# A relational graph network on one core: 128 counted nodes in the first layer, and all counted products in one pass over the row blocks

## The chip, the core and the metric

The kernel runs on one core of a Trainium2 chip. Its engines work side by side and meet at semaphores: TensorE (PE in the profile) multiplies, VectorE (DVE) and ScalarE (ACT) work element by element, GpSimd (POOL) issues the gathers, and SyncE (SP) issues most other transfers. [...]The metric is the device time of one execution in microseconds.

## The reference, cut to what matters

```
src, dst, type: 100000 edges; dst = int(6250 * u^2), sorted; x: 6250 x 256
for l in range(3):                        # W_rel[l]: 8 x 256 x 256
    xr  = einsum('nd,rde->rne', x, W_rel[l])
    agg = segment_sum(xr[type, src], dst, 6250)
    x   = relu(agg + x @ W_root[l] + bias[l])
x = layernorm(x_in + x)
x = layernorm(x + attention(x, edges))    # four heads, the attention runs at the end
```

A layer sums, for each node and each of the 8 relations, the rows of the edges that arrive there, and multiplies the sums by that relation's weights. Because `dst` is a square of a uniform number, nodes with low numbers get very many edges: the first 64 nodes get about 10,100 of the 100,000, the first 128 about 14,300, the first 192 about 17,500.

## The kernel before, in words

**Edges in tiles.** The 782 tiles of 128 sorted edges are worked off in groups of four, one group per step of the loop at the end of `layer`, from the last tile down to the first. Tiles above and below `TM` are interleaved and have two separate accumulators `S[0]` and `S[1]` (rings of node tiles, f = 0 and f = 1). In a step, `gather` (L577) lets POOL fetch the source rows of four tiles into one of the seven buffers of `msg` (rows split into three bf16 parts; in the first 32 steps of layer zero, unsplit f32); `onehot` (L557) compares keys on DVE; `windows` (L597) multiplies rows by one-hots on PE into a window of W nodes by 8 relations; `add` (L609) adds the windows to `S` on DVE at a place read at run time. When a node tile of 128 nodes has all its edges (the table `ready` says after which step), `dense` (L664, L668) multiplies its sums by the weights: 18 f32 matmuls, which the trace records as 36, dealt out a few per step, or one node tile per step once the groups are used up. `finish` adds the bias, applies relu, and stores the row block twice, as f32 (L703) and as three bf16 parts (L706). The next layer's gathers take any row, so they start after the last store.

**Hot nodes are counted.** For the first `HOTS[l]` nodes of a layer (64, 192, 192) no edge is gathered; the tiles that hold only such edges are skipped. `starts` and `count` build instead, for 64 nodes at a time (a chunk), a table of how many edges come from each row under each relation: per pair of a node and 128 of its edges, a compare on DVE (L897; every fourth pair one more, L893), a matmul (L905), and per node a copy by ACT to the byte array `A` (L908). The table is written to device memory (`cnts`, L914). `products` then multiplies all rows of the layer by the counts: 13 row blocks of up to 512 rows, per chunk two products (k = 0, 1) of eight matmuls of 512 columns (L993), rows split into two parts `top` and `rest` (L976 on ACT, L977 on DVE), counts cast to f32r by ACT (L981), and a sum on DVE (L960). A row block is loaded (L949) into a buffer of `msg`, the pool of the gathers.

**Where this work stands.** `jobs` is a generator that the loop asks up to three times a step (`work(0)` ahead of the gather, `work(1)` after the windows, `work(2)` after the adds). What it yields names the places at which it may go on; at HEAVY, a product is given out only where the planner's tally of PE time lies below 5 us times the step, or where the products left outnumber 0.9 times the steps left to `last_step`:

```
def light(i):
    return spent[0] < STEP * i + SLACK or left[0] > 0.9 * (last_step - i)
last_step = (PREP_AT if final else NG) - 12
```

Layer zero counts chunk 0 (steps 44 to 97), does its 26 products (98 to 134, straight from `A`), then counts chunk 1 (150 to 183, past its last group). Layer one counts chunk 2 (12 to 34) and does 78 products in two passes, chunks 0 and 1 first and then chunk 2, which loads and splits every row block twice (39 to 153). Layer two does the same two passes (10 to 141). Node tile 0 has no gathered edges in layers one and two; its dense work then comes at `ready[1, 1] - 2`, two steps before the last group.

Of the kernel before, what the change touches and what calls it, by code (L numbers as in the profile page):

```python
# [29 lines left out]
PAD = 32  # L30
MARGIN = 800
CHUNK = 64
HOTS = (64, 192, 192)
PASSES = ((0, 1), (2,))
FIRST = 32
SELS = 6
LOWS = 3
# [138 lines left out]
def fast(tc, const, pl, x, xs, xb, src, dst, edge_type, w_rel, w_root, bias, weight,  # L176
# [10 lines left out]
    with ExitStack() as top:  # L187
# [35 lines left out]
        with ExitStack() as s:  # L223
            wp = s.enter_context(tc.tile_pool(name="wp", bufs=1))
            sp = s.enter_context(tc.tile_pool(name="sp", bufs=1))
            xp = s.enter_context(tc.tile_pool(name="xp", bufs=3))
            hp = s.enter_context(tc.tile_pool(name="hp", bufs=1))
            ps_w = s.enter_context(tc.tile_pool(name="ps_w", bufs=4, space=PSUM))
            ps_d = s.enter_context(tc.tile_pool(name="ps_d", bufs=1, space=PSUM))
            ps_h = s.enter_context(tc.tile_pool(name="ps_h", bufs=2, space=PSUM))  # L230

            mp = s.enter_context(tc.tile_pool(name="mp", bufs=7))
            op = s.enter_context(tc.tile_pool(name="op", bufs=AHEAD + 2))

# [43 lines left out]
def tables(tc, pl, ps_t, src, dst, edge_type, ident, idx, key, pos, iota, iota_p, lane, edges, hd,  # L278
# [5 lines left out]
    with tc.tile_pool(name="prep", bufs=1) as prep:  # L284
# [120 lines left out]
        masked = prep.tile([P, 64], F32, name="masked")  # L405
        for h, k, t0, t1 in (
                (HOTS[-1], key1, pl.THS[-1], pl.K1),
                (HOTS[0], key[:, pl.TH:pl.bands[0][1]], pl.TH, pl.bands[0][1])):
# [114 lines left out]
def layer(tc, pl, l, final, groups, ready, S, hold, A, hd, key1, edges, cnts, flag, idx, key, pos, iota,  # L523
# [303 lines left out]
    def count(chunk, pace=ALL):  # L827
# [58 lines left out]
        for m in range(len(pairs) + SELS - 2):  # L886
# [14 lines left out]
            if m >= SELS - 2:  # L901
# [4 lines left out]
                if i == rows_[n] - 1:  # L906
# [20 lines left out]
    def products():  # L927

        B = GT
        C = CHUNK * R  # L930
        assert C == 512
        loads = [range(a, min(a + B, NT)) for a in range(0, NT, B)]
        sums = hp.tile([P, 2, KC, C], F32, name="sums")
        room = A.rearrange("p j s -> p (j s)")
        more = room[:, :4 * KC * C].bitcast(F32).rearrange("p (k c) -> p k c", k=KC)
        kept = [room[:, 4 * KC * C + i * 2 * B * C:4 * KC * C + (i + 1) * 2 * B * C] for i in range(2)]
        held_ = {}

        def load(m, cs):
            js = loads[m]  # L940
            t = mp.tile([P, GT, 3 * D], BF16, name="msg").rearrange(
                "p q d -> p (q d)").bitcast(F32)[:, :B * D].rearrange("p (q d) -> p q d", d=D)
            full = len(js) if js[-1] < NT - 1 or LAST == P else len(js) - 1
            if full < len(js):
# [6 lines left out]
            for u, c in enumerate(cs if l else ()):  # L951
                nc.sync.dma_start(kept[m % 2][:, u * B * C:u * B * C + len(js) * C],
                                  cnts[c][:, js[0] * C:(js[-1] + 1) * C])
            return t

        def add_up(m, o, ph):
            if m == 0:
                nc.vector.tensor_copy(o, ph[:, :C])
            else:
                nc.vector.tensor_tensor(o, o, ph[:, :C], ALU.add)  # L960

        for cs in PASSES:
            cs = [c for c in cs if c < HOT // CHUNK]
            if not cs:
                continue
            for c in cs:
                held_[c] = sums[:, c] if c < 2 else more
            ts = {0: load(0, cs)}
            yield from pause(3)
            yield MID  # L970
            last = None
            for m, js in enumerate(loads):
                g = len(js)
                t = ts.pop(m)
                top, rest = buffer(0, F32R, B * D), buffer(1, F32R, B * D)
                nc.scalar.copy(top[:, :g * D], t[:, :g].rearrange("p t d -> p (t d)"))  # L976
                nc.vector.tensor_tensor(rest[:, :g * D], t[:, :g].rearrange("p t d -> p (t d)"),  # L977
                                        top[:, :g * D], ALU.subtract)
                for u, c in enumerate(cs):
                    cn = buffer(2, F32R, B * C)  # L980
                    nc.scalar.copy(cn[:, :g * C], kept[m % 2][:, u * B * C:u * B * C + g * C] if l  # L981
                                   else room[:, js[0] * C:(js[-1] + 1) * C])
                    if u == 0 and m + 1 < len(loads):
                        ts[m + 1] = load(m + 1, cs)
                    for k in range(KC):
                        if last:
                            yield END
                            add_up(*last)
                        yield HEAVY
                        ph = ps_h.tile([P, 512], F32, name="ph")  # L990
                        for n in range(g):
                            for part in (top, rest):
                                nc.tensor.matmul(  # L993
                                    ph[:, :C], part[:, n * D + k * P:n * D + (k + 1) * P],
                                    cn[:, n * C:(n + 1) * C], start=(n == 0 and part is top),
                                    stop=(n == g - 1 and part is rest))
                        last = m, held_[c][:, k], ph
                        left[0] -= 1
                    yield MID
            add_up(*last)  # L1000
            yield HEAD
        while not {3, 4} <= set(cleared):
            yield HEAD
        for c, v in held_.items():
            j, at = divmod(c * CHUNK, P)
            for k in range(KC):
                o = cols(1, j)[:, k * R:(k + 1) * R, at:at + CHUNK]
                nc.vector.tensor_tensor(
                    o, o, v[:, k].rearrange("p (n r) -> p r n", r=R), ALU.add)
        summed.append(True)  # L1010
        yield HEAD

# [722 lines left out]
```

## Time and profile before

| | us |
|---|---|
| median of three runs (lowest, highest) | 3454.05 (3449.44, 3460.27) |
| the profiled execution, its own time | 2871.54 |
| its span, first to last instruction | 2869.7 |
| PE / DVE / POOL / ACT busy in the span | 2503.9 / 1925.6 / 1955.1 / 847.7 |
| mean granted PE clock | 0.945 |

The profile is of one execution, and its time is well below the median of the runs; durations below are those of the profiled execution. A group in the profile has its line, engine and operation, the tile written and the tiles read, the number of instructions, the busy time, the mean of one in ns, and then the idle time of the engine before them with what ended it. A timeline row gives the start, the length, the engine, the line, and in brackets the idle time before it.

### The profile page before, as it was taken

To read this page: it belongs to the slowest core of one execution; us is meant where nothing else is said; L and a number is where in the kernel's file an instruction comes from. 1 tells how busy PE (TensorE), PEld (TensorE's weight loads), DVE (VectorE), ACT (ScalarE), POOL (GpSimd) and SP (SyncE) were. 2 spreads that over 40 slices of the span, in tenths; PEclk is the share of its full clock that TensorE was granted. 3 is DMA by queue.
4 is the path that set the end of the run, shared out by engine and by line. 5 is a ranking of instruction groups with operands and counts; after the bars stand their busy time and mean duration, and the time that the engine had idled before them with its cause. 6 is when DMAs were issued, how large, how long until landed. Compare 5 with 4: busy or idle time off the path is not lost.

```text
span 2869.7 us, 55366 instructions
## 1 busy us (share of the span) xinstructions
PE 2503.9 (87%) x20054; PEld 2168.5 (76%) x20055; DVE 1925.6 (67%) x4564; ACT 847.7 (30%) x1178; POOL 1955.1 (68%) x2026
## 2 busy tenths in 40 slices
PE   2899999999766689999999998789999999998775
PEld 1788778787655578888888877678888888877664
DVE  6776888767655468666666766367666665767858
ACT  2332223333123224332333342212222232232014
POOL 5657777777777477677777777477767766667701
PEclk8999999999989799999999999899999999999885
DMA  5756666766666666767676776566656665666724
GB/s 156 229 189 184 191 187 185 237 212 212 177 183 176 198 176 189 244 201 213 211 229 210 216 249 201 156 211 179 199 176 190 195 202 171 215 200 195 236 71 159
DMA packets 245854, 560.53 MB, mean 195 GB/s; under 512 B 43533, under 2 KB 124452, under 8 KB 245188
## 3 DMA queue, kind: packets, MB, share of 16 engines
q0 software_dynamic: 126656, 387.18, 46.3%
q1 hardware_dynamic: 115720, 166.95, 17.0%
q8 instruction: 161, 2.64, 0.4%
q10 hardware_dynamic: 3196, 2.76, 0.3%
q14 instruction: 121, 0.99, 0.1%
HBM read 492.51 MB, written 64.21 MB: 194 GB/s over the span
## 4 chain that ended last, share of the span: by engine, by line
PE 60%; DVE 12%; issue 8%; DMA 7%; POOL 6%; ACT 5%; SPq 2%; DVEq 1%; ACTq 0%; POOLq 0%
PE pd L668 27%; PE pw L597 16%; PE ph L993 10%; POOL msg L577 6%; DMA msg<-xb,idx 4%; PE pd L664 4%; DVE S L609 3%; ACT S L682 1%; ACT u L981 1%; PE pw L641 1%; SPq L850 1%; PE ph L905 1%; DMA u<-in_x_dram 1%; DVE oh L557 1%; DMA u<-in_dst_dram 1%
## 5 line engine op out<-in xcount | busy, mean ns | idle before, releaser
L577 POOL DMA_INDIRECT msg<-xb,idx x1886 | 1823.4, 967 | 704.0 <-issue 536.4
L668 PE MATMUL pd<-wr,S 128*128 128x256 f32 x4800 | 1123.2, 384 | 1.6 <-DVE S L650 1.1
L609 DVE TENSOR_TENSOR S<-S,pw 128x320 f32 (+21 forms) x2010 | 848.7, 422 | 391.8 <-PE pw L597 262.8
L668 PEld LDWEIGHTS pd<-wr,S 128*128 128x128 f32 x4800 | 904.8, 192 | 119.3 <-DVE S L650 2.1
L597 PE MATMUL pw<-oh,msg 128*128 128x160 bf16 (+20 forms) x11316 | 746.3, 224 | 150.7 <-DMA msg<-xb,idx 124.6
L597 PEld LDWEIGHTS <-msg 128*128 128x128 bf16 x11316 | 679.7, 101 | 245.9 <-DMA msg<-xb,idx 149.7
L993 PE MATMUL ph<-u,u 128*128 128x512 f32 x1372 | 380.1, 418 | 36.6 <-ACT u L981 36.3
L557 DVE TENSOR_TENSOR oh<-iota,key 128x640 bf16<-128x640 f32 (+19 forms) x475 | 319.4, 673 | 16.4 <-issue 12.4
L993 PEld LDWEIGHTS ph<-u,u 128*128 128x128 f32 x1372 | 256.3, 193 | 92.4 <-ACT u L981 41.4
L682 ACT ACTIVATE S<-S 128x2048 uint32<-128x2048 uint32 x150 | 284.5, 1896 | 4.3 <-PE pd L668 2.6
L644 ACT COPY xT<-pw 128x256 f32<-128x256 f32 x195 | 71.8, 371 | 682.2 <-PE pw L641 682.2
L664 PE MATMUL pd<-wo,xT 128*128 128x256 f32 x588 | 168.4, 411 | 27.0 <-DVE h L710 20.2
L981 ACT CAST u<-A 128x2048 fp32r<-128x2048 uint8 (+1 forms) x91 | 163.5, 1797 | 50.4 <-PE ph L993 38.7
L577 POOL DMA_INDIRECT msg<-in_x_dram,idx x124 | 120.3, 970 | 77.4 <-issue 31.7
L908 ACT CAST A<-ph 128x392 uint8<-128x392 f32 x192 | 90.9, 485 | 272.4 <-PE ph L905 268.2
L698 ACT ACTIVATE hb<-h 128x256 bf16<-128x256 f32 x98 | 41.1, 419 | 413.5 <-DVE h L697 413.5
L977 DVE TENSOR_TENSOR u<-msg,u 128x1024 fp32r<-128x1024 f32 (+1 forms) x65 | 75.6, 1163 | 130.4 <-ACT u L976 130.3
L664 PEld LDWEIGHTS pd<-wo,xT 128*128 128x128 f32 x588 | 107.5, 200 | 43.9 <-DVE h L710 22.5
L597 PE MATMUL pw<-A,msg 128*128 128x120 f32 (+5 forms) x496 | 85.8, 330 | 29.0 <-DVE S L609 21.6
L716 ACT ACTIVATE rs<-mv,eps 128x1 f32<-128x1 f32 x49 | 14.4, 295 | 309.0 <-DVE mv L715 308.0
L597 PEld LDWEIGHTS pw<-A,msg 128*128 128x128 f32 x496 | 78.7, 207 | 34.9 <-DVE S L609 24.9
L976 ACT CAST u<-msg 128x1024 fp32r<-128x1024 f32 (+1 forms) x65 | 64.5, 992 | 135.0 <-PE ph L993 110.3
(246 smaller groups left out, 1458.7 us busy)
## 6 DMA issues: line engine op xcount, KB each, us to landing
msg<-xb,idx POOLq DMA_INDIRECT x1886
msg<-x SPq DMA_DIRECT2D x48, 512.0 KB
xb<-hb SPq DMA_DIRECT2D x96, 192.0 KB
A<-cnts SPq DMA_DIRECT2D x72, 256.0 KB
x<-h SPq DMA_DIRECT2D x96, 128.0 KB
xin<-x SPq DMA_DIRECT2D x96, 128.0 KB
cnts<-A SPq DMA_DIRECT2D x3, 3136.0 KB
xb<-u SPq DMA_DIRECT2D x24, 384.0 KB
```

What stands on the lines that cost most here:

```text
L557: nc.vector.tensor_tensor(oh[:, :len(g), :w], iota[:, :w].unsqueeze(1).to_broadcast([P, len(g), w]), kk.unsqueeze(2).to_broadcast([P, len( ...
L577: nc.gpsimd.indirect_dma_start(out=msg[:, q, :], out_offset=None, in_=xb[l] if split(i) else table, in_offset=bass.IndirectOffsetOnAxis(ap ...
L597: nc.tensor.matmul(pw[:, k * w:(k + 1) * w], msg[:, q, o:o + P], oh[:, q, :w], start=(c == 0), stop=(c == parts - 1))
L609: ins = nc.vector.tensor_tensor(o, o, pw.rearrange("p (a b) -> p a b", b=W), ALU.add)
L644: nc.scalar.copy(xT.rearrange("p k n -> p (k n)"), pt[:, :D])
L664: nc.tensor.matmul(pd[:, :D], xT[:, k], wo[:, k], start=(k == 0), stop=False)
L668: i = nc.tensor.matmul(pd[:, :D], s[:, k * R + r], wr[:, k, r], start=(xT is None and k == r == 0), stop=(k == KC - 1 and r == R - 1))
L682: i = nc.scalar.memzero(cols(f, j))
L908: nc.scalar.copy(A[:, :, c * R:(c + 1) * R], pc[:, :NT * R].rearrange("p (j r) -> p j r", r=R))
L977: nc.vector.tensor_tensor(rest[:, :g * D], t[:, :g].rearrange("p t d -> p (t d)"), top[:, :g * D], ALU.subtract)
L981: nc.scalar.copy(cn[:, :g * C], kept[m % 2][:, u * B * C:u * B * C + g * C] if l else room[:, js[0] * C:(js[-1] + 1) * C])
L993: nc.tensor.matmul(ph[:, :C], part[:, n * D + k * P:n * D + (k + 1) * P], cn[:, n * C:(n + 1) * C], start=(n == 0 and part is top), stop=( ...
```

## The change

Layer zero counts 128 nodes (two chunks) before its products, which are 52 in place of 26; it skips 36 tiles more, and has 169 groups in place of 179. All layers read the counts back from device memory, and the sums lie in `A` too. `products` goes once over the 13 row blocks with all chunks of the layer; the cast of the next unit (a row block and a chunk) is issued between the two products of the present one, into two alternating buffers, and the next row block is loaded two products before it is split (`split_rows`: `top` on ACT, `rest` on DVE, as before). Before, a row block was loaded right after the split of the one ahead of it. `count` goes on by two pairs per yield. The dense work of node tile 0 in layers one and two comes at `ready[1, 3] + 6`. The products' deadline is `ready[1, 1]` or `ready[1, 3]`, whichever the last line below picks, with a factor 1.2. `TM`, which halves the tiles, moves with the smallest number of skipped tiles; layers one and two then have 163 groups in place of 164, of the same 650 tiles.

```diff
-HOTS = (64, 192, 192)
-PASSES = ((0, 1), (2,))
+HOTS = (128, 192, 192)
...
-                        ready[1, 0] = ready[1, 1] - 2
+                        ready[1, 0] = ready[1, 3] + 6
...
-            yield pace
+            if m % 2:
+                yield pace
...
+        units = [(m, c) for m in range(len(loads)) for c in cs]
+        sums = [room[:, c * 4 * KC * C:(c + 1) * 4 * KC * C].bitcast(F32).rearrange(
+            "p (k c) -> p k c", k=KC) for c in cs]
...
+        def load_counts(m):
+            js = loads[m]
+            for c in cs:
+                nc.sync.dma_start(kept[m % 2][:, c * B * C:c * B * C + len(js) * C],
+                                  cnts[c][:, js[0] * C:(js[-1] + 1) * C])
...
+        def cast(n):
+            m, c = units[n]
+            g = len(loads[m])
+            cn = cns[n] = buffer(2 + n % 2, F32R, B * C)
+            nc.scalar.copy(cn[:, :g * C], kept[m % 2][:, c * B * C:c * B * C + g * C])
...
-        for cs in PASSES:
...
+        load_counts(0)
+        load(0)
+        yield from pause(3)
+        yield MID
+        split_rows(0)
+        cast(0)
+        for n, (m, c) in enumerate(units):
+            more = m + 1 < len(loads)
+            yield HEAVY
+            ph = multiply(n, 0)
+            yield MID
+            if c == 0 and more:
+                load_counts(m + 1)
+            if n + 1 < len(units):
+                cast(n + 1)
+            yield END
+            add_up(n, 0, ph)
+            yield HEAVY
+            ph = multiply(n, 1)
+            yield MID
+            if c == len(cs) - 2 and more:
+                load(m + 1)
+            if c == len(cs) - 1 and more:
+                split_rows(m + 1)
+            yield END
+            add_up(n, 1, ph)
+            if c == len(cs) - 1 and not late_hot(step[0]):
+                yield HEAD
...
-            yield from chain(starts(0), count(0), products(), starts(1, (0, 1)), count(1, (0, 1)))
-        elif l == 1:
-            yield from chain(starts(2), count(2), products())
-        else:
-            yield from pause(6)
-            yield from products()
+        for c in range(HOTS[l - 1] // CHUNK if l else 0, HOT // CHUNK):
+            yield from starts(c)
+            yield from count(c)
+        yield from products()
...
-        return spent[0] < STEP * i + SLACK or left[0] > 0.9 * (last_step - i)
+        return spent[0] < STEP * i + SLACK or late_hot(i)
+
+    def late_hot(i):
+        return left[0] * 1.2 > last_step - i
...
-    last_step = (PREP_AT if final else NG) - 12
+    last_step = ready[1, 1] if ready[1, 1] < ready[1, 0] else ready[1, 3]
```

More of the change, by code (lines that the diff above doesn't have):

```diff
@@ L407, in tables @@
                 (HOTS[-1], key1, pl.THS[-1], pl.K1),
-                (HOTS[0], key[:, pl.TH:pl.bands[0][1]], pl.TH, pl.bands[0][1])):
+                (HOTS[0], key[:, pl.THS[0]:pl.bands[HOTS[0] // CHUNK - 1][1]], pl.THS[0],
+                 pl.bands[HOTS[0] // CHUNK - 1][1])):
             m = masked[:, :t1 - t0]
@@ L931, in products, with load @@
         assert C == 512
+        cs = range(HOT // CHUNK)
         loads = [range(a, min(a + B, NT)) for a in range(0, NT, B)]
-        sums = hp.tile([P, 2, KC, C], F32, name="sums")
+        units = [(m, c) for m in range(len(loads)) for c in cs]
         room = A.rearrange("p j s -> p (j s)")
[L935 to L939, printed above, removed]
-            js = loads[m]
-            t = mp.tile([P, GT, 3 * D], BF16, name="msg").rearrange(
+        sums = [room[:, c * 4 * KC * C:(c + 1) * 4 * KC * C].bitcast(F32).rearrange(
+            "p (k c) -> p k c", k=KC) for c in cs]
+        at = len(cs) * 4 * KC * C
+        kept = [room[:, at + i * len(cs) * B * C:at + (i + 1) * len(cs) * B * C] for i in range(2)]
+        ts, cns, tops = {}, {}, {}
+        def load_counts(m):
+            js = loads[m]
+            for c in cs:
+                nc.sync.dma_start(kept[m % 2][:, c * B * C:c * B * C + len(js) * C],
+                                  cnts[c][:, js[0] * C:(js[-1] + 1) * C])
+        def load(m):
+            js = loads[m]
+            t = ts[m] = mp.tile([P, GT, 3 * D], BF16, name="msg").rearrange(
                 "p q d -> p (q d)").bitcast(F32)[:, :B * D].rearrange("p (q d) -> p q d", d=D)
@@ L950, in load, with split_rows, multiply, add_up @@
                     "(p t) d -> p t d", p=P))
[L951 to L956, printed above, removed]
+        def split_rows(m):
+            g = len(loads[m])
+            t = ts.pop(m)
+            top, rest = tops[m] = buffer(0, F32R, B * D), buffer(1, F32R, B * D)
+            nc.scalar.copy(top[:, :g * D], t[:, :g].rearrange("p t d -> p (t d)"))
+            nc.vector.tensor_tensor(rest[:, :g * D], t[:, :g].rearrange("p t d -> p (t d)"),
+                                    top[:, :g * D], ALU.subtract)
+        def cast(n):
+            m, c = units[n]
+            g = len(loads[m])
+            cn = cns[n] = buffer(2 + n % 2, F32R, B * C)
+            nc.scalar.copy(cn[:, :g * C], kept[m % 2][:, c * B * C:c * B * C + g * C])
+        def multiply(n, k):
+            m, c = units[n]
+            ph = ps_h.tile([P, 512], F32, name="ph")
+            g = len(loads[m])
+            for i in range(g):
+                for part in tops[m]:
+                    nc.tensor.matmul(
+                        ph[:, :C], part[:, i * D + k * P:i * D + (k + 1) * P],
+                        cns[n][:, i * C:(i + 1) * C], start=(i == 0 and part is tops[m][0]),
+                        stop=(i == g - 1 and part is tops[m][1]))
+            left[0] -= 1
+            return ph
+        def add_up(n, k, ph):
+            m, c = units[n]
+            o = sums[c][:, k]
             if m == 0:
@@ L960, in add_up @@
                 nc.vector.tensor_tensor(o, o, ph[:, :C], ALU.add)
-        for cs in PASSES:
[L963 to L969, printed above, removed]
-            yield MID
[L971 to L1001, printed above, removed]
@@ L1002, in products @@
         while not {3, 4} <= set(cleared):
             yield HEAD
-        for c, v in held_.items():
+        for c in cs:
             j, at = divmod(c * CHUNK, P)
@@ L1008, in products @@
                 nc.vector.tensor_tensor(
-                    o, o, v[:, k].rearrange("p (n r) -> p r n", r=R), ALU.add)
+                    o, o, sums[c][:, k].rearrange("p (n r) -> p r n", r=R), ALU.add)
         summed.append(True)
```

## The prediction

> **What bounds the kernel now.** I read the page's busy times and groups first, then the gathers in order of time, then stages of the layers, then who ended POOL's and PE's waits. The page has three engines near full:
>
> ```profile
> PE 2503.9 (87%) x20054; PEld 2168.5 (76%) x20055; DVE 1925.6 (67%) x4564; ACT 847.7 (30%) x1178; POOL 1955.1 (68%) x2026
> L577 POOL DMA_INDIRECT msg<-xb,idx x1886 | 1823.4, 967 | 704.0 <-issue 536.4
> L993 PE MATMUL ph<-u,u 128*128 128x512 f32 x1372 | 380.1, 418 | 36.6 <-ACT u L981 36.3
> ```
>
> The timeline of POOL in layer two shows what the 68% hide:
>
> ```profile
> 2119.22 0.94 POOL L577 DMA_INDIRECT msg<-xb,idx  x1 [0.30 <-issue]
> 2120.47 0.94 POOL L577 DMA_INDIRECT msg<-xb,idx  x1 [0.30 <-issue]
> ...
> 2128.56 0.94 POOL L577 DMA_INDIRECT msg<-xb,idx  x1 [7.14 <-PE pw L597]
> ```
>
> A gather follows a gather after 1.25 us, 5.0 us per step of four. [...]2010 tiles by 1.25 is 2512 of the 2870 us. It breaks where a gather waits for the windows (L597) that read its buffer: PE is then a full ring of `msg` behind. The stages, each with its steps (POOL's instructions over four):
>
> ```profile
> core 0: us, PE busy (x) PEld busy (x) DVE busy (x) ACT busy (x) POOL busy (x), PEclk, DMA share, GB/s
> 298.00:552.00 254.00, 236.38 (x2038) 202.61 (x2038) 211.94 (x534) 80.73 (x144) 191.74 (x200) 0.99 0.64 187
> 564.00:735.00 171.00, 161.61 (x1326) 137.25 (x1323) 110.78 (x232) 61.36 (x68) 130.51 (x132) 0.98 0.69 215
> 735.00:949.00 214.00, 151.14 (x1498) 126.35 (x1498) 122.55 (x335) 53.41 (x98) 162.22 (x171) 0.89 0.62 178
> 1170.00:1760.00 590.00, 570.04 (x4594) 491.30 (x4591) 381.16 (x792) 201.41 (x231) 443.21 (x457) 0.99 0.72 222
> 2249.00:2611.00 362.00, 341.08 (x2717) 292.41 (x2714) 234.76 (x528) 114.35 (x116) 245.82 (x253) 0.98 0.64 198
> ```
>
> PE per step: 4.73 us while layer zero counts (50 steps), 4.90 in its products (33), 3.54 in its rest (43), 4.99 in layer one's products (114), 5.39 in layer two's (63). So the gathers bound the end of layer zero, and PE bounds layers one and two: 590 us for 114 steps and 362 for 63 are 20 and 46 us over the pace. The waits of POOL in layer two and of PE in layers one and two:
>
> ```profile
> POOL msg L577 <- PE pw L597: 62.3, 46, 7.1
> ...
> PE ph L993 <- ACT u L981: 18.5, 9, 5.5
> ...
> PE ph L993 <- ACT u L981: 13.8, 8, 4.0
> ```
>
> Last, PE's end of layer one: two node tiles run alone, at 8.6 us each, before layer two's gathers may start.
>
> ```profile
> 1823.66 1.13 PE L664 MATMUL pd<-wo,xT 128*128 128x256 f32 x4 [0.52 <-DVE h L697]
> 1824.63 7.07 PE L668 MATMUL pd<-wr,S 128*128 128x256 f32 x32
> 1832.31 1.10 PE L664 MATMUL pd<-wo,xT 128*128 128x256 f32 x4 [0.61 <-DVE h L697]
> 1833.25 7.07 PE L668 MATMUL pd<-wr,S 128*128 128x256 f32 x32
> ```
>
> [...]I take pitches from starts (a mean of 418 ns for L993 stands against 2.08 us for eight in the timeline). [...]The median is 3454.05/2871.54 = 1.203 times the profiled execution[...]; no run shows the clock of the timed runs. I work on the profiled execution and scale by 1.203.
>
> **Layer zero.** Removed: 36 tiles x 1.25 = -45 us of gathers. Their windows are among PE's narrowest, 40 and 48 columns (24 matmuls in 0.77 us near 952), so PE loses only about 6 us; the 36 adds and 9 one-hots are DVE's. Added: 26 products x 2.08 = +54 us of PE. SP gets 26 loads of counts (256 KB each), POOL loses 36 gathers; the DMA queues were busy 0.62 to 0.72 of the time, so this stays hidden, and if it didn't, a late load would hold one product, 2 us.
> Counting runs at six pairs a step in place of three, in 26 steps (44 to 70) for chunk 0 and 11 (83 to 94) for chunk 1. DVE was at 211.94/50 = 4.24 us a step; three more pairs are 3 x (0.23 for L897 by its pitch + a quarter of 0.60 for L893) = 1.15, with reductions and small waits about 5.7. PE gets 3 x 0.17 more, 5.2. So 26 x 0.7 = 18 us behind the pace. Around step 50 the windows start 21 us after their gathers end; with seven buffers POOL stops at about 28 (seven steps of 5 less the landing and the windows). 5 to 7 us are free, so about +13 stall. Steps 71 to 82 are light and win some back; chunk 1's counts take it again.
> Products from step 97 to 145, one in each step. PE's other work is (161.6 - 24.5 x 2.08)/33 = 3.35, with the product 5.43: 0.43 x 48 = 21 us behind, on a lag of some 25: +17 stall. In all +30. After step 149 PE has slack and the gathers set the pace.
> End: before, node tile 1 was done ten steps early; now tiles 0 and 1 both become ready after the last group: +8.6 us alone on PE. Chunk 1's count and its 3 MB write, which stood in this tail, are gone: -2. Sum: -45 + 30 + 6.6 = -8.
>
> **Layer one.** The same tiles and products. The deadline moves from step 152 to 140: 73 products in 97 steps in place of 114. Other work (570 - 72 x 2.08)/114 = 3.69, plus 1.57, is 5.26 a step; the casts come one unit ahead, so I drop PE's waits for ACT (18.5 us) and leave 0.07 of waits: 97 x 0.33 = 32 us behind, of which 28 - 15 = 13 are covered, so 19 to 30 of stall against the 20 before: +8. The freed PE time after step 140 is worth nothing there, as POOL bounds it. 13 splits and loads fewer (1.0 us of ACT, 1.2 of DVE, 512 KB each) are hidden by PE's 5.2 us a step; uncovered, they would be worth up to 15 us, as the low end below has it. A row block's load now waits on SP for the buffer of the gathers six steps back, and the `xin` loads and the stores queue behind it; they are needed three steps later, and PE is past those windows by then, so it costs nothing (one late `xin` cost PE 5.4 us in this layer before). The six sums into `S` (L1008, 1.08 us each) fall at step 145, when PE has slack. Node tile 0 is done at step 146, so only one node tile is left at the end: -8.6. Sum: -1.
>
> **Layer two.** Products start at step 3, in the idle PE of the layer's start, about four earlier: -8. Waits for casts 13.8, of which I take 10. A row block held one of the seven buffers nearly all the time before; now two steps in seven, so POOL may run a step further ahead: -5, once. That is 23; a load still takes a buffer at times, so -21. Node tile 0 again leaves the tail: -8.6. Sum: -30.
> A count's write to device memory is now waited for in layer zero as it was in layer one (5.5 us at the first product); three steps of pause cover it.
>
> **Sum:** -8 - 1 - 30 = -39 us, the profiled execution at 2832 us; times 1.203, -47 us: **3407 us**.
>
> **What is not shown.** Six pairs a step: from 5.3 us a step (no stall, -13) to 6.6 (PE, DVE and ACT waiting for each other over two PSUM banks, +25). Casts ahead: from nothing gained (+24 over both layers) to all waits gone, layer zero's 4.0 too (-8). Layer one's deadline: from -10, if the splits and loads matter, to +20.
>
> **The rivals.**
> *A, the counting stage hides and the ring absorbs it.* For it: DVE at 4.24, free PSUM after 71. Against: the lag at step 50 is near the limit already. Layer zero then gives -38, the sum is about -70 in the profile: 3370.
> *B, slower: PE becomes the bound of layer zero.* It gains 48 us of PE net and the gathers' 45 us saving is only worth something while PE has slack; layer zero has it after step 134 alone (3.54 of 5.0). If counting takes 6.6 us a step and products 5.7, layer zero comes out at +25; with 20 more of stall and its shorter tail layer one gives +11, and layer two, without the gain on casts, -20: +16, or 3473. It decides from about 6.3 us a step in the counting stage, where the first layer's 45 us are used up.
> *C, no change worth measuring:* casts ahead gain nothing, as ACT was late only 36 us in all and POOL bounds when PE is early; sum within 8 us.
>
> **How the numbers follow.** Mine 0.50 (-20 to -55 us), A 0.25, B 0.14, C 0.11. A measurement can tell about 0.3%, 10 us of the median. Faster 0.77, within 0.10, slower 0.13. The range takes in A to its middle and the mild half of C: 3362 to 3458; my case alone 3388 to 3430.
>
> **What would show it.** Right: POOL's pitch 1.25 as before, layer zero shorter by some 8 us from first gather to next layer's first, with POOL waits on windows between its steps 55 and 70; L993's wait for L981 nearly gone; a first-gather gap of about 28 us ahead of layer two in place of 36.5, and about 34 ahead of layer one. Wrong: no waits in the counting stage (A), or gathers waiting all through layers zero and one (B), or a new wait of PE for the split rows.

## The result, and the profile after

| | us |
|---|---|
| before, median of 4 runs (lowest, highest) | 3457.16 (3449.44, 3461.17) |
| after, median of 4 runs (lowest, highest) | 3412.82 (3400.28, 3413.18) |
| after / before | 0.9866, 95% interval 0.9836 to 0.9895 |

The changed kernel is faster by 44 us; the forecast was 3407. One plain fact has to come before any line of the profiles. The kernel before takes about 3450 us in these runs and 3451 and 3413 us in the first two sets of experiments, but 2877 and 2873 us in the last two, which is as long as in the profile that the forecast was made on. I call the chips of these sets the long and the short chips. No chip stands in two of the sets of experiments, so whether it is the chip or a state that it was in is not shown. The change is worth the same share on both, but its microseconds lie in different places, so I compare profiles only within one kind.

**The short chips**, where the sum was made. The changed kernel was profiled there too (run e13_after, below). Its page, the lines that answer to those of before:

```profile
span 2834.7 us, 55098 instructions
PE 2533.8 (89%) x20030; PEld 2193.1 (77%) x20031; DVE 1909.5 (67%) x4522; ACT 843.9 (30%) x1165; POOL 1913.8 (68%) x1990
L577 POOL DMA_INDIRECT msg<-xb,idx x1848 | 1776.0, 961 | 729.0 <-issue 516.4
L982 PE MATMUL ph<-u,u 128*128 128x512 f32 x1568 | 428.4, 414 | 9.9 <-ACT u L974 4.7
```

The products (L982, which was L993) are 1568 matmuls in place of 1372, and wait for casts 4.7 us in place of 36.3. The span went from 2869.7 to 2834.7: **35.0 us less**, where the forecast's sum says 39. The stages, cut at POOL's steps (columns: length, busy time of each engine, granted clock, then the DMA queues' share and rate; PEld is TensorE's loading of weights):

```profile
core 0: us, PE busy (x) PEld busy (x) DVE busy (x) ACT busy (x) POOL busy (x), PEclk, DMA share, GB/s
268.00:421.00 153.00, 138.50 (x1107) 117.15 (x1105) 131.77 (x333) 49.08 (x90) 103.34 (x108) 0.98 0.58 168
421.00:563.00 142.00, 126.39 (x1086) 105.59 (x1083) 114.95 (x293) 54.48 (x107) 99.50 (x106) 0.98 0.65 198
563.00:849.00 286.00, 275.28 (x2198) 231.80 (x2197) 180.82 (x396) 108.96 (x122) 201.14 (x209) 0.99 0.70 222
2339.00:2590.00 251.00, 246.44 (x2030) 212.85 (x2028) 166.79 (x389) 74.53 (x79) 181.60 (x188) 1.00 0.64 194
```

Two of the same stages before, the first and the last of these:

```profile
268.00:405.00 137.00, 123.99 (x1030) 107.15 (x1028) 108.56 (x259) 34.39 (x58) 102.87 (x108) 0.99 0.65 188
2342.00:2611.00 269.00, 250.06 (x1991) 213.45 (x1989) 174.55 (x393) 86.81 (x88) 183.90 (x188) 0.98 0.64 200
```

In the table after, the first row is the counting of chunk 0, 27 steps (44 to 71): 5.68 us a step (before 5.09), with all engines below 91%. The second holds chunk 1 (26 steps, 5.43), the third layer zero's products (52 steps, PE at 96%), the last the second half of layer two's products (47 steps, 5.34; before some 5.7). From the starts of the gathers in the two traces, stage by stage; "over pace" is the time beyond 1.25 us a tile, and all but the first row are us:

| | before | after | difference | forecast |
|---|---|---|---|---|
| layer zero: number of tiles up to its last step (difference in us, at 1.25 a tile) | 706 | 670 | -45 | -45 |
| steps 0 to 44, over pace | 41.6 | 39.8 | -1.8 | 0 |
| steps 44 to 71 (chunk 0 counted) | 2.4 | 18.2 | +15.8 | +13 |
| steps 71 to 97 (chunk 1 counted) | 1.5 | 11.1 | +9.6 | 0 |
| steps 97 to 149 (products) | 9.3 | 26.4 | +17.1 | +17 |
| rest, and the end up to layer one's first gather | | | +5.7 | +6.6 |
| layer one, over pace | 26.4 | 35.1 | +8.7 | +8 |
| its end, last gather to layer two's first | 32.7 | 25.0 | -7.7 | -8.6 |
| layer two, over pace | 67.4 | 41.4 | -26.0 | -21 |
| its tail, last gather to the end | 143.7 | 133.1 | -10.6 | -8.6 |

The traces' first gathers differ by 0.4 us too, and together this makes the 35. POOL's wait for windows in layer two (before, 62.3 us; total, times, longest):

```profile
POOL msg L577 <- PE pw L597: 39.5, 41, 3.7
```

And the timeline of PE at the end of layer one, in the same run:

```profile
1828.23 5.43 PE L668 MATMUL pd<-wr,S 128*128 128x256 f32 x24
1834.27 1.10 PE L664 MATMUL pd<-wo,xT 128*128 128x256 f32 x4 [0.61 <-DVE h L697]
1835.21 7.07 PE L668 MATMUL pd<-wr,S 128*128 128x256 f32 x32
```

One node tile stands alone on PE now (1834 to 1842); before there were two.

**The long chips**, where the result was measured. The page of after there:

```profile
span 3410.9 us, 55098 instructions
PE 2748.9 (81%) x20030; PEld 2301.6 (67%) x20031; DVE 1900.8 (56%) x4522; ACT 846.4 (25%) x1165; POOL 1909.0 (56%) x1990
L577 POOL DMA_INDIRECT msg<-xb,idx x1848 | 1773.7, 960 | 1264.0 <-issue 520.2
L982 PE MATMUL ph<-u,u 128*128 128x512 f32 x1568 | 450.3, 428 | 14.2 <-issue 4.8
```

A gather lasts 960 ns on the long chip and 961 on the short one; the idle time before the gathers is 1264 us and 729. Work on DVE and ACT doesn't last longer either, 1900.8 us of DVE against 1909.5 and 846.4 of ACT against 843.9; these engines wait longer.

### The profile page after: what moved, and what is told of

It is laid out like the page before. It is cut to its first block, busy times and chain, and to the rows that moved or that the text cites. A ratio compares the mean times of both kernels' runs of the same rounds, so it can differ in the third digit from the quotient of the medians.

```text
span 3410.9 us, 55098 instructions
## 1 busy us (share of the span) xinstructions
PE 2748.9 (81%) x20030; PEld 2301.6 (67%) x20031; DVE 1900.8 (56%) x4522; ACT 846.4 (25%) x1165; POOL 1909.0 (56%) x1990
## 4 chain that ended last, share of the span: by engine, by line
PE 40%; DVE 8%; issue 6%; another core or an unknown queue 4%; ACT 2%; POOL 1%; DMA 1%; SPq 0%; DVEq 0%; POOLq 0%; ACTq 0%
PE pd L668 18%; PE pw L597 11%; PE ph L982 6%; PE pd L664 3%; DVE S L609 2%; POOL msg L577 1%; PE pw L641 1%; DMA msg<-xb,idx 1%; DVE oh L557 1%; ACT S L682 1%; PE pw L736 1%; DVE ga L1091 0%; DVE st L1414 0%; DVE z L1402 0%
## 5 line engine op out<-in xcount | busy, mean ns | idle before, releaser
L577 POOL DMA_INDIRECT msg<-xb,idx x1848 | 1773.7, 960 | 1264.0 <-issue 520.2
L609 DVE TENSOR_TENSOR S<-S,pw 128x320 f32 (+17 forms) x1974 | 840.5, 426 | 968.4 <-remote 419.9
L668 PE MATMUL pd<-wr,S 128*128 128x256 f32 x4800 | 1201.0, 401 | 31.0 <-issue 25.1
L597 PE MATMUL pw<-oh,msg 128*128 128x160 bf16 (+18 forms) x11088 | 809.9, 230 | 343.6 <-issue 161.5
L982 PE MATMUL ph<-u,u 128*128 128x512 f32 x1568 | 450.3, 428 | 14.2 <-issue 4.8
L982 PEld LDWEIGHTS ph<-u,u 128*128 128x128 f32 x1568 | 300.0, 198 | 80.5 <-issue 12.2
L644 ACT COPY xT<-pw 128x256 f32<-128x256 f32 x195 | 72.0, 372 | 1043.0 <-PE pw L641 400.8
L557 DVE TENSOR_TENSOR oh<-iota,key 128x640 bf16<-128x640 f32 (+20 forms) x463 | 315.3, 682 | 15.7 <-issue 12.4
L974 ACT CAST u<-A 128x2048 fp32r<-128x2048 uint8 (+1 forms) x104 | 186.6, 1795 | 53.4 <-issue 21.1
L698 ACT ACTIVATE hb<-h 128x256 bf16<-128x256 f32 x98 | 40.9, 417 | 634.8 <-DVE h L697 413.9
L995 DVE TENSOR_TENSOR A<-A,ph 128x512 f32<-128x512 f32 x192 | 130.5, 680 | 0.0
L597 PE MATMUL pw<-A,msg 128*128 128x200 f32 (+5 forms) x504 | 95.7, 347 | 34.1 <-DVE S L609 15.6
L905 PE MATMUL ph<-u 128*128 128x392 bf16 x284 | 75.5, 339 | 27.4 <-ACT A L908 12.5
```

Of the source, the lines that this page charges most:

```text
L557: nc.vector.tensor_tensor(oh[:, :len(g), :w], iota[:, :w].unsqueeze(1).to_broadcast([P, len(g), w]), kk.unsqueeze(2).to_broadcast([P, len( ...
L577: nc.gpsimd.indirect_dma_start(out=msg[:, q, :], out_offset=None, in_=xb[l] if split(i) else table, in_offset=bass.IndirectOffsetOnAxis(ap ...
L597: nc.tensor.matmul(pw[:, k * w:(k + 1) * w], msg[:, q, o:o + P], oh[:, q, :w], start=(c == 0), stop=(c == parts - 1))
L609: ins = nc.vector.tensor_tensor(o, o, pw.rearrange("p (a b) -> p a b", b=W), ALU.add)
L668: i = nc.tensor.matmul(pd[:, :D], s[:, k * R + r], wr[:, k, r], start=(xT is None and k == r == 0), stop=(k == KC - 1 and r == R - 1))
L905: nc.tensor.matmul(pc[:, :NT * R], low, oh, start=(i == 0), stop=(i == rows_[n] - 1))
```

## The experiments

**1. The kernel before on a long chip (e0_before).** No edit.

> The kernel before, unchanged, profiled a second time: it is to be compared with the profile after in an execution that lasts as long as the timed runs. If the factor of 1.203 that I put between the profiled execution and the median is a lower clock of all engines, the gathers of L577, 960 ns in the profile after, must be about as long here as there and the span about 3455 us, but then 967 ns in the execution of 2871 us speaks against a clock already. If it is something that makes PE late (instructions that come late, a lower granted clock), each operation of POOL, DVE and ACT lasts as long as in the execution of 2871 us, and the mean step is longer than 6 us because PE has idle time in it.

3454.58 us, span 3452.8. Three groups of its page:

```profile
L577 POOL DMA_INDIRECT msg<-xb,idx x1886 | 1825.6, 968 | 1247.9 <-issue 527.2
L609 DVE TENSOR_TENSOR S<-S,pw 128x320 f32 (+21 forms) x2010 | 850.0, 423 | 915.3 <-remote 372.1
L668 PE MATMUL pd<-wr,S 128*128 128x256 f32 x4800 | 1205.7, 402 | 37.4 <-issue 30.0
```

Two lines of its waits (total, times, longest; PEld loads weights):

```profile
PEld L597 <- issue: 438.1, 515, 18.9
...
DVE S L609 <- remote: 372.1, 170, 13.9
```

Against the execution of 2871 us (967 ns, 422 ns and 384 ns for the same three groups, and 73.1 us for that first wait) only PE's matmuls are a little longer, 5%, with a granted clock of 0.887 in place of 0.945. So the factor of 1.203 isn't a clock that all engines share. The timeline of POOL shows where it comes from:

```profile
1447.44 0.94 POOL L577 DMA_INDIRECT msg<-xb,idx  x1 [1.58 <-PE pd L668]
1448.69 0.95 POOL L577 DMA_INDIRECT msg<-xb,idx  x1 [0.30 <-issue]
1449.94 0.95 POOL L577 DMA_INDIRECT msg<-xb,idx  x1 [0.30 <-issue]
1451.19 0.95 POOL L577 DMA_INDIRECT msg<-xb,idx  x1 [0.30 <-issue]
1453.55 0.94 POOL L577 DMA_INDIRECT msg<-xb,idx  x1 [1.41 <-PE pw L641]
```

Within a step the pitch is 1.25 us as ever. The first gather of a step, the one that waits for PE, comes 2.32 us after the gather before it (median of 504 steps; 1.25 on the short chip). In all, first gathers are late by 643 us here and by 112 in the execution of 2871 us: 532 of the 583 us between the two. And what waits for PE waits on after PE is done, as the timeline of all engines has it:

```profile
1302.12 0.49 PE L905 MATMUL ph<-u 128*128 128x392 bf16 x2
...
1305.38 0.87 ACT L908 CAST A<-ph 128x392 uint8<-128x392 f32 x2 [2.83 <-remote]
...
1305.91 0.33 PE L905 MATMUL ph<-u 128*128 128x392 bf16 x1 [2.58 <-issue]
```

ACT copies a count out of PSUM over 2 us after the last matmul that it can have waited for, and PE waits for the free bank. Over the trace, ACT's copies L644 that found ACT idle start over 0.3 us after the end of the matmul of L641 in 31% of cases here, and in none of 142 on the short chip; ACT's copies L698, which wait for DVE, start within 0.04 us on both. So on the long chips it is PE's releases (the semaphore updates that other engines wait for) that come late. The labels "remote" and "issue" are no evidence of another core or of late instructions: this trace holds 22014 semaphore records, that of 2871 us has 51720, so the releaser's record is often missing.

The same trace narrows this further, since it records the updates of PE's semaphore themselves. On the short chip an update stands 14 ns (median) after the recorded end of its matmul. So it does here wherever no gather runs, at the ends of the two layers and in the tail: 105 of 105 matmuls find an update within 15 ns. In the stretch with gathers, 60% of the matmuls find none within 0.3 us (1% on the short chip); a ninth of PE's updates have no record, which can account for a part of this only. Gathers were running at 60% of the ends of these matmuls, but at 33% of the updates (71% and 70% on the short chip). Once there is an update, ACT's late copies start 0.02 us behind it, and in 40 of their 44 cases PE had begun other matmuls in between. So the update is late, not PE's work, and it is late only where POOL gathers; all nine traces of long chips have this. The granted clock is not the reason: where the full clock was granted, first gathers still come 2.30 us after the one ahead (median of 297). That the gathers hold the updates up is a reading of such times; no run on a long chip took gathers away. How they would do it, and why on these chips alone, stays open.

From this run and the profile of after on a long chip, the 42 us there: layer zero up to layer one's first gather 1166.4 to 1146.1 (-20), layer one up to layer two's 1088.6 to 1071.3 (-17), layer two and the tail 1186.4 to 1182.4 (-4). Five profiles of the changed kernel and of variants that change layer two little or not at all differ by up to 7 us in its gathers (1034.6 to 1042.0), so a layer's number is good to some 7, and the 4 us are not told from nothing.

**2. Layer zero as before (e1_hot64).** 64 nodes in layer zero, chunk 1 counted after its products; all else as changed.

```diff
-HOTS = (128, 192, 192)
+HOTS = (64, 192, 192)
...
+            if len(cs) == 1 and more:
+                load(m + 1)
...
-        for c in range(HOTS[l - 1] // CHUNK if l else 0, HOT // CHUNK):
+        for c in ((0,), (2,), ())[l]:
...
+        if l == 0:
+            yield from starts(1)
+            yield from count(1)
```

> The changed kernel, with 64 counted nodes in layer zero again and chunk 1 counted after the products of layer zero, as before. My forecast: counting 128 nodes and the node tile that is left over give layer zero -8 us in the profile, -10 in a timed run, so this kernel takes about 3423 us, 10 more than the changed one. Rival A (the counting hides, 36 tiles of gathers are saved in full): 45 x 1.2 more, 3458. Rival B (PE bounds layer zero, which loses by the products): less than the changed kernel, about 3385 to 3400.

3437.63 us, ratio to before 0.9950 (0.9931 to 0.9969). Against 0.9866 for the changed kernel, counting 128 nodes is worth 0.8%, 29 us of the 44, on a long chip. By the two intervals that is 17 to 41 us, between my forecast (10) and rival A (45, or 54 with the factor of 1.2 that its text names). Its first layer took 1175.7 us up to layer one's first gather, 30 more than the changed kernel's.

**3. Node tile 0 late, as before (e3_tile0_late).**

```diff
-                        ready[1, 0] = ready[1, 3] + 6
+                        ready[1, 0] = ready[1, 1] - 2
```

> The changed kernel, with the dense work of node tile 0 in layers one and two back at two steps before the last group. My forecast: one node tile of 8.6 us more runs alone on PE at each of the two ends, 17 us in the profile and 20 in a timed run: 3433 us. If the node tile's end was hidden or PE is behind anyway, nothing: 3413 within 5.

3419.65 us (3402.10 to 3438.06), ratio 0.9891 (0.9849 to 0.9934), which can't be told from 0.9866. Its profile shows the two ends as forecast, 58.4 us from the last gather to layer two's first (49.7 with the change) and a tail of 161.1 (147.7), 22 us together (the profile is of the slowest of its four runs). The time doesn't confirm that, nor does it speak against it, since its interval spans 29 us.

**4. One pass alone (e4_one_pass_only).** The kernel before with all chunks in one pass.

```diff
-PASSES = ((0, 1), (2,))
+PASSES = ((0, 1, 2),)
...
-        kept = [room[:, 4 * KC * C + i * 2 * B * C:4 * KC * C + (i + 1) * 2 * B * C] for i in range(2)]
+        kept = [room[:, 4 * KC * C + i * 3 * B * C:4 * KC * C + (i + 1) * 3 * B * C] for i in range(2)]
```

> The kernel before, with all three chunks of layers one and two in one pass over the row blocks and nothing else changed: 26 loads and splits of row blocks fewer, casts of counts still right before their products, 64 nodes in layer zero. My forecast put nothing on the loads and splits themselves (PE's work hides them): about 3457 us, the time before, within 6. Rival: the splits on ACT and DVE and the buffer of the gathers that each row block takes matter, 15 us in layer one and as much in layer two, times 1.2: about 3421.

3477.29 us, ratio 1.0079 (1.0056 to 1.0102): 27 us slower. Both the forecast (no change) and its rival (a gain) missed; that the single pass loses was in no theory. What 26 loads and splits fewer are worth can't be read from it. By its profile the loss is not in layer one, which goes over the rows in the same way (1088.8 us to layer two's first gather; 1088.6 in run 1), but in layer two and its tail (1203.5; 1186.4). Two of its differences from the new form were then put back one at a time, the late casts (6, below) and the early loads (9), and neither is large enough alone; both together weren't tried, so why it loses 27 stays open.

**5. Half of each product left out (e5_no_rest), a third of the windows' matmuls left out (e6_two_parts).** The first multiplies only the top parts of the rows, the second only two of the three bf16 parts; the rest of the program is as changed.

```diff
-                for part in tops[m]:
+                for part in tops[m][:1]:
...
-                        stop=(i == g - 1 and part is tops[m][1]))
+                        stop=(i == g - 1))
```
```diff
-                parts = 3 if split(i) else 1
+                parts = 2 if split(i) else 1
```

> The changed kernel with half of each product left out: only the top parts of the rows are multiplied by the counts, not the rest parts; casts, splits, loads, sums and their waits all stay. PE has 196 x 1.03 = 200 us less to do. Theory new since the first four runs: in executions as long as the timed ones, what PE releases reaches ACT, DVE and POOL late, and the steps of some 6.3 us are made of such waits and not of PE's work; then most of the 200 us is not gained: 3340 to 3413 us. Rival, on which my forecast's products and deadlines rest: PE's work bounds the stages with products: 150 to 200 us less, 3210 to 3260.

> The changed kernel with the third of the three bf16 parts of each gathered row left out of the windows (the gathers fetch it still): 3700 matmuls, a third of the 810 us of L597, so PE has up to 270 us less to do over all stages, in as many windows, adds and steps. Theory of the late releases: little of it is gained, 3330 to 3413 us. Rival, PE's work bounds: 200 to 270 us less, 3140 to 3210. Theory that the gathers' pace of 5.0 us a step bounds: nothing, 3413.

Ratios to before on their (long) chip 0.9821 (0.9789 to 0.9852) and 0.9751 (0.9726 to 0.9775); before was 3412.5 us there. Against 0.9866 that is 0.45% and 1.15%, about 15 and 39 us. What was taken from PE is read from the pages. That of e5_no_rest:

```profile
L982 PE MATMUL ph<-u,u 128*128 128x512 f32 x784 | 260.5, 453 | 16.6 <-issue 4.5
```

That of e6_two_parts:

```profile
L597 PE MATMUL pw<-oh,msg 128*128 128x160 bf16 (+18 forms) x7392 | 573.4, 231 | 340.3 <-issue 118.3
```

By the recorded times PE had 190 and 237 us less to do (450.3 and 809.9 in the changed kernel on a long chip), and of that some twelfth and a sixth came off the whole time. So on the long chips PE's amount of work is not what bounds most steps; run 1 has them waiting for its late releases. My forecast's reason for the products' stalls, that PE has more than 5 us of work in a step, is seen on the short chips alone.

**6. Casts not ahead (e7_cast_late).** The cast moves from between the two products of the unit before to right before its own first product.

```diff
             if c == 0 and more:
                 load_counts(m + 1)
-            if n + 1 < len(units):
-                cast(n + 1)
...
+            if n + 1 < len(units):
+                cast(n + 1)
             yield END
             add_up(n, 1, ph)
```

> The changed kernel with each cast of counts issued right before its first product, as in the kernel before, in place of one unit ahead; one pass, two buffers. My forecast took 10 us of waits in layer two and 18 in layer one as gained by the casts ahead, 28 x 1.2: about 3445 us. That the one pass alone lost 26 us in the run before this one says as much: 3435 to 3445. Rival C (casts ahead gain nothing): 3413 within 6.

Ratio 0.9874 (0.9856 to 0.9892): nothing lost that shows; by the intervals at most some 15 us, where the forecast for this run had 32. Its list of PE's waits has the wait for casts back,

```profile
PE ph L982 <- ACT u L974: 40.2, 16, 4.6
```

against 4.2 us in the changed kernel's on a long chip. So a wait of 40 us cost little or nothing there: PE is not short of time on a long chip.

**7. Four pairs counted per step (e2_four_pairs).**

```diff
-            if m % 2:
+            if m % 4 != 3:
```

> The changed kernel with four pairs counted in a step in place of six, so that layer zero's counting lasts some 16 steps longer and its 52 products stand closer together. My forecast put a stall of 13 us on six pairs a step; four keep DVE under 5 us a step, which takes most of that away, 13 x 1.2 = 15 us, but the products then fall due at more than one a step, and I put 15 to 25 us on that: 3405 to 3430. Rival: at over 6 us a step the counting hides at either speed and so do the products, 3413 within 6.

Ratio 0.9871 (0.9832 to 0.9911), no difference from six pairs that shows. On a long chip these steps last 6.2 us in the kernel before too, so this says nothing of the stall that the short chip shows (18.2 us in steps 44 to 71).

**8. Every second gather issued by SP (e9_half_gathers).** In the split steps, plain transfers of 128 rows (other rows than the edges name).

```diff
+            if split(i) and q % 2:
+                nc.sync.dma_start(msg[:, q, :], xb[l][i * P % 6016:i * P % 6016 + P, :])
+                continue
```

> The changed kernel with every second gather of the split steps replaced by a plain transfer of 128 other rows that SP issues: as many bytes land in msg, and PE, DVE and ACT have the same work (the rows are the wrong ones). POOL issues two gathers in a step, 2.5 us in place of 5.0. Theory since the first eight runs: in executions as long as the timed ones PE's signals are held while POOL issues gathers and come through in the pause of about 1 us behind the fourth, so a step lasts 5.0 + 1.05 us at the least; here the floor falls to about 3.6 us and PE's own 4.9 to 5.4 us bounds: 480 steps shorter by 0.8 to 1.2 us, 2850 to 3030 us. Rival: PE's signals are late for a reason that has nothing to do with POOL's gathers: no gain, 3350 to 3420, as the half of a product left out gained little. Rival: the gathers' bytes bound: no gain either.

3644 us where the kernel before took 2877: it fell on a short chip, where PE's releases are not late, so it doesn't test what it was made for. It ran into another wait, the longest of PE's:

```profile
PE pw L600 <- DMA msg<-xb: 726.5, 159, 22.5
```

PE waited 726 us for SP's transfers. SP itself waited 1183 us in this trace for the rows that it was to store (L706 there, which is L703 in the changed kernel); that the transfers came late because they stand behind such waits in SP's order is likely, not tested. So the test of whether POOL's gathers hold up PE's releases on the long chips is still to be made; run 1's trace speaks for it by its times alone.

**9. Row blocks loaded early, as before (e10_load_early), and gathers issued two groups at a time (e12_paired).**

```diff
+        load(1)
         cast(0)
...
-            if c == len(cs) - 2 and more:
-                load(m + 1)
             if c == len(cs) - 1 and more:
                 split_rows(m + 1)
+                if m + 2 < len(loads):
+                    load(m + 2)
```
```diff
+    msgs = {}
...
-            msg = gather(i)
+            if i % 2 == 0:
+                for k in range(i, min(i + 2, NG)):
+                    msgs[k] = gather(k)
+            msg = msgs.pop(i)
```

> The changed kernel with each row block loaded right after the split of the one ahead of it, as before, so that it holds one of the seven buffers of the gathers nearly all the time of the products. My forecast: 5 us in layer two, once, and none in layer one, as the ring fills once: 3413 + 6. Rival: the buffer is what made the one pass alone slower than two by 26 us: 25 to 35 us more than the changed kernel.

> The changed kernel with the gathers of two groups issued one after the other in every second step. Nothing is left out. Theory that PE's signals come through only in POOL's pauses: pauses come half as often. If the pause is the only price, (8 x 1.25 + 1.05)/2 = 5.5 us a step in place of 6.05, 250 us less, 3160; if DVE's adds, which need PE's signal for each window and free the four PSUM banks, then get through half as often, the steps grow and it is slower than the changed kernel, 3500 or more. Rival, signals late for another reason: within 30 us of the changed kernel, as only one buffer of the ring is taken earlier.

Both on a short chip: 2844.80 us, ratio 0.9894 (0.9869 to 0.9919), and 2840.55, ratio 0.9881 (0.9852 to 0.9910). The changed kernel has 0.9868 on another short chip (run 10). So the late load is worth some 8 us, give or take 10: the forecast's 5, or nothing, and not the 25 to 35 of the rival. Where it lies was forecast otherwise: against run 10's profile layer one is 5 us longer up to the next layer's first gather (876.8; 871.4) and layer two with its tail no longer (984.5; 985.8), and I had put the 5 us on layer two. Pairing makes no difference that shows; for late releases it was no test.

**10. The changed kernel on a short chip (e13_after).** No edit.

> The changed kernel itself, unchanged, profiled a second time and timed against the kernel before. If the chip is one on which the kernel before takes about 2875 us, as in the profile that my sum was made on: the sum says 39 us less, 0.986, of which layer zero -8, layer one -1, layer two -30; the kernel with early loads took 0.989 there, so the late load is worth 0 to 10 us. If it is one on which the kernel before takes 3410 to 3460: 0.985 to 0.989 again, and in the profile the gap ahead of layer two and the tail some 10 us each shorter than before, layer zero 20 us shorter and the gathers of layer two no shorter at all.

2836.89 us against 2872.97, ratio 0.9868 (0.9846 to 0.9890). The stages are in the table above: layer zero +1.3, layer one +1, layer two with its tail -36.7.

## Why the prediction was right, step by step

**The sum** of -39 us is -35 on a chip like that of the execution that it was made for, and all its terms but one came out within 5 us. Some of that is luck: layer zero fell 9 us short of its forecast, and layer two beat its own by 7. The median, for which 3407 was forecast, was 3412.82; that this came out has another reason than the forecast's, as the part on the scale says.

**Layer zero.** Counting at 5.7 us a step with +13 of stall: 5.68 and +15.8, and the wait stood where it was put, from step 56 on. The reason for 5.7 is confirmed only in part: I had DVE at 5.39 us of work a step and PE at 5.2; by the table DVE was busy 4.88 and PE 5.13, so it is the waits between them that are larger than I thought. POOL waits there for PE, mostly with a count's matmul as PE's last work (waits of POOL in the changed kernel on the short chip, 268 to 421 us):

```profile
POOL msg L577 <- PE ph L905: 18.3, 12, 4.7
POOL msg L577 <- PE pw L597: 4.3, 7, 2.1
```

In the kernel before the two were 0.3 and 1.2 us over the same steps. Products +17: +17.1. The step that failed is "Steps 71 to 82 are light and win some back; chunk 1's counts take it again", which put that stretch at nothing: it cost 9.6 us. Part of it stands at steps 74 and 79, where PE was still a full ring behind from chunk 0; the longest wait, 5.8 us, is step 95's, as the first row block takes a buffer: that gather starts at 552.5, right after the windows of six steps back have ended (552.3), not seven (546.8). I had let the row blocks' buffers cost nothing in layer zero. The same happens at step 100 (7.2 us), within the products' 17. So layer zero gave +1.3 in place of -8, which is nothing that can be told from zero. The 36 tiles saved are all paid back in stalls, as rival B has it, but its +25 was not reached. Rival A, that counting hides, is out on the short chip.

**Layer one.** +8.7 of stall for +8, and -7.7 at the end for -8.6: +1 for -1. The +8 did not follow from its own working: 19 to 30 us of stall against 20 before is -1 to +10, with +4.5 in the middle, and the stall of the whole layer before was 26.4.

**Layer two.** -26 of stall for -21, -10.6 for -8.6 in the tail. I took 10 of the 13.8 us of waits for casts; in the profile after, no such wait is listed in layer two. The gain lies mainly in the second half of the products (some 18 of the 26). How it divides among casts, the earlier start and the buffers was argued and not tested apart on a short chip, except the early load, which cost layer two nothing (run 9); so the 5 us that I put on the buffer are not found there.

**The scale of 1.203.** Its number served, the idea behind it did not. I let all times of the profiled execution grow alike by the bare ratio of the median to it, as if all engines shared a slower clock; that was an estimate, and no trace had shown such a clock. Then every engine's operation would read longer, and gathers (967 and 968 ns), adds (422 and 423 ns) and casts of counts (1797 ns in the kernel before on the short chip, 1795 in the changed kernel on a long one) don't. It is late releases of PE, about 1.07 us in the median step (2.32 less 1.25). That the ratio is the same on both kinds of chip, 0.9866 and 0.9868, is then no consequence of my argument, and that the median came within 6 us of 3407 is luck: on the long chips the change gains 20 us in layer zero, where I had 10, 17 in layer one, where I had 1, and 4 in layer two with its tail, where I had 36. In layer zero ten steps fewer (179 - 169, of 6.29 us each, the mean before) are 63 us, against longer steps (169 x 0.19 = 32 us, as the mean rose to 6.48) and the longer end (12 us). That what spares PE work or waits counts for little there fits runs 5 to 7. Of the 17 us of layer one, 10 lie in its gathers and 7 in its end (56.8 to 49.7 us); why the gathers gained was not tested.

**What would have shown it.** The pitch of 1.25, the waits from step 56 on and the vanished wait for casts were as written. Layer zero was not 8 us shorter. Counted from the first gather of the last step, as the forecast did, the gap ahead of layer two was 29 us for 28, and ahead of layer one 32 for 34.

## What to carry to other kernels

Before a profile and a median that differ by 20% are put together by a factor, profile the same program again where it is slow and compare the mean duration of each group: if they agree, it is waits that grew, and a change that spares busy time need not scale (in run 5, 190 us less of PE's work took some 15 us off the time). A sum made stage by stage against a pace that did not change (here POOL's 1.25 us a gather) held to within 5 us in all its terms but one, where it was measured on the kind of chip that it was made for. Two kernels that differ by the same percentage on two chips may do so for different reasons; say which stage it came from on each.

## What the runs showed of the hardware

Chips, or their states, differ by a factor of 1.2 for this program: the kernel before took 3451 and 3413 us on two and 2877 and 2873 on two others. On the long ones operations of POOL, DVE and ACT last as long (a gather 968 ns against 967, an add on DVE 423 against 422, ACT's casts of counts 1795 in the changed kernel against 1797), PE's granted clock is 0.887 in place of 0.945, and releases by PE come late (ACT's L644: over 0.3 us late in 31% of its waits in run 1, in none of 142 on the short chip; in run 1's timeline a copy starts over 2 us late), while ACT's L698 starts 0.03 us after DVE's L697 on both. The late ones stand only in the stretches in which POOL gathers; at the layers' ends and in the tail, PE's updates follow within 15 ns on both kinds of chip (105 of 105 matmuls in run 1, 74 of 74 in the profile before).

No gather followed another in less than 1.24 us in the traces of the two kernels, on either kind of chip (1.244 us at the least in the profile before, 1.245 in that of after on a long chip).
